# Keys in one written order, the output bias copied by ScalarE, low-rank products and step sizes with features on partitions, and an earlier loop entry, in a twelve-layer decoder kernel

## The chip, the cores and the metric

The kernel runs on one core of a Trainium2 chip. The time is that of the device for one launch, in microseconds (us); the profiled execution is one launch recorded instruction by instruction. The core has TensorE (PE; its weight loads are listed apart as PEld), VectorE (DVE), ScalarE (ACT), GpSimd (POOL) and SyncE (SP), each with a queue that it works off in order. They wait for one another by semaphores. All data are float32 if nothing else is said.

## The reference, cut to what matters

The program is a decoder of four blocks of three layers (attention, cross attention to a context, feed-forward), with a layer norm ahead of each layer and x = x + layer(norm(x)). x is 8 batches of 128 tokens by 256 features, the context 8 by 128 by 128. The change touches four layers: the third block's three and the fourth block's attention.

Third block, attention (`L2_attn`): a recurrence over tokens, with a rate for each head.

```python
q, k = elu(xWq) + 1, elu(xWk) + 1
kv_t = decay * kv_{t-1} + k_t * v_t ; ks_t = decay * ks_{t-1} + k_t
out = (q * kv / clip(sum_head(q * ks), 1e-6)) @ w_out
```

Third block, cross attention (`L2_xattn`): 16 heads of 16; the last 16 tokens of the context have weights and biases of their own and a softmax of their own; queries and keys are layer-normed by head.

```python
k = _ln((y_main @ Wk + bk).reshape(..., H, HD), kn_w, kn_b)
k_dca = _ln((y_dca @ Wk_dca + bk_dca).reshape(..., H, HD), kn_dca_w, kn_dca_b)
ctx = _attn(q, k, v) + _attn(q, k_dca, v_dca)
return ctx @ Wo + bo
```

Third block, feed-forward (`L2_ffn`): a base product, a shared product of rank 16 and six routed ones of rank 16, two of which count for a token.

```python
gates = softmax(x @ W_router + b_router) ; top two kept as w_per_e
h = einsum('bsd,edr->bser', x, A_r) * w_per_e[..., None]
return x @ W_base + b_base + (x @ A_s) @ B_s + einsum('bser,erf->bsf', h, B_r)
```

Fourth block, attention (`L3_attn`): a state space layer with 64 heads of 64 and a state of 128. z, x, B, C and dt are products of the normed input; x, B and C pass a causal convolution of four taps and a silu.

```python
dt = softplus(dt + dt_bias) ; dA_cs = cumsum(dt * A) over 128 tokens
L[i, j] = exp(dA_cs[i] - dA_cs[j]) for j <= i
Y = einsum('bcign,bcjgn,bcijgh,bcjghp->bcighp', Cm, Bm, L, dt * x) + D * x
return rmsnorm(Y * silu(z)) * norm_w @ W_out
```

## The kernel before, in words

x lies in SBUF as 128 tokens (partitions) by 8 batches by 256 features. A norm works in two halves of four batches: `norm_stats` (L144) takes statistics on VectorE, has ScalarE do a Ln and an Exp for the inverse root (L125, L126), corrects it in three small VectorE steps (L129 to L131) and writes `xn` (L165). `norm` (L172) turns `xn` with TensorE into `xnT` (features on partitions) and copies it out of PSUM, by turns with ScalarE and VectorE (L60, L62). `add_x` (L191) adds a result to x on VectorE.

Two things set the order of work. Inside `manual_schedule` (and so in `in_step`, L376) the instructions of each engine keep the order written down; outside of it, a planner orders them by its own costs, and it may mix them between those of written orders. `in_step` runs a list of stages, each with a lag, over blocks.

*Keys of the cross attention* (`L2Keys.keys`, L1521) are made at the end of the first feed-forward layer with experts (`l1_ffn`), while its last results come back from memory (y, L1298). There are two written orders: `Decay` and `rest` (parameters turned to columns, the value bias passed through Wo to `bo`), then four rounds of `project` (TensorE; ScalarE copies with bias, L1555, and squares, L1617), sums by head on TensorE, Ln and Exp (L1623, L1624), and `scaled`, a multiply on GpSimd (L1562). After them, outside of a written order, VectorE adds y to x and norms it. `masked` and `values` come later, in the steps of `l2_attn` (`late`).

*Recurrence* (`l2_attn`): four steps (two halves by two groups of features), each with three products, the scans on VectorE (L1392, L1393) by the rates of `Decay`, sums by head (L1412), inverse, spread (L1427) with `feats`, output.

*Cross attention* (`l2_xattn`): eight blocks through a pipeline of stages. `bias` (L1759) adds `bo` to x on GpSimd; it needs only that the norm has read x.

*Low-rank feed-forward* (`l2_ffn`, L1770): norm, with the base bias added to x by GpSimd (L188); router; softmax; `top2`; then for each of eight blocks a product x by A (128 tokens by 112), its weighting on VectorE (L1801), a transpose, a copy, and base product and low-rank product into one bank. It has no written order.

*State space layer* (`l3_attn`, L1817): norm, then one written order. The entry (L2014 to L2097) computes the step sizes with tokens on partitions (eight times two matmuls of 64 columns), softplus by Abs, Exp, Ln, Exp, a cumulative sum as a matmul with a triangle, a turn of the sums, their split into three bfloat16 parts, and writes the parts to memory (`parts`, L2057) to read them back as `own` (L2062) and, two blocks at a time, `upto` (L1912, `sums`); `decay` (L1917) then has TensorE form the differences and ScalarE bring them to SBUF. Beside that B and C are projected, convolved (`last_tap` on ScalarE, three `taps` on VectorE) and multiplied (`gT`), and the first two feature blocks are prepared. The loop (L2102) then runs fifteen passes over pairs of blocks. PSUM has two banks each with the names xz (products, differences) and ty (turns, results), and four with the name o.

## Time and profile before

| what | value |
|---|---|
| median of 3 runs | 1963.13 us (1957.91 to 1964.25) |
| profiled execution | 1960.42 us, span 1958.6 us |
| granted TensorE clock, mean of the span | 0.943 |
| busy: PE, DVE, ACT, POOL | 1712.1, 1203.2, 1034.0, 376.1 us |

By stage, from the busy times in stretches of the trace (us):

| stretch | what runs | PE | DVE | ACT | POOL | clock |
|---|---|---|---|---|---|---|
| 885 to 905 | keys, y added, norm | 12.0 | 14.6 | 8.8 | 8.1 | 0.83 |
| 905 to 940 | recurrence | 33.2 | 27.7 | 22.4 | 2.6 | 1.00 |
| 940 to 972 | its end, queries | 20.3 | 19.7 | 11.3 | 6.0 | 1.00 |
| 1000 to 1060 | cross attention | 53.4 | 39.4 | 32.9 | 3.0 | 1.00 |
| 1060 to 1103 | low-rank feed-forward | 33.6 | 25.4 | 6.0 | 9.7 | 0.80 |
| 1103 to 1145 | entry of the state space layer | 35.9 | 22.5 | 21.4 | 2.6 | 0.88 |
| 1200 to 1250 | its loop | 49.8 | 33.1 | 37.5 | 0.0 | 1.00 |

A line of the timeline gives start, duration, engine, line, operation, output<-inputs, shapes, how many were merged, and in brackets how long the engine stood idle before it and for whom. A matmul in float32 appears as two records.

### The profile page before, as it was taken

To read this page: it belongs to the slowest core of one execution; us is meant where nothing else is said; L and a number is where in the kernel's file an instruction comes from. 1 tells how busy PE (TensorE), PEld (TensorE's weight loads), DVE (VectorE), ACT (ScalarE), POOL (GpSimd) and SP (SyncE) were. 2 spreads that over 40 slices of the span, in tenths; PEclk is the share of its full clock that TensorE was granted. 3 is DMA by queue.
4 is the path that set the end of the run, shared out by engine and by line. 5 is a ranking of instruction groups with operands and counts; after the bars stand their busy time and mean duration, and the time that the engine had idled before them with its cause. 6 is when DMAs were issued, how large, how long until landed. Compare 5 with 4: busy or idle time off the path is not lost.

```text
span 1958.6 us, 25273 instructions
## 1 busy us (share of the span) xinstructions
PE 1712.1 (87%) x9521; PEld 1136.4 (58%) x9527; DVE 1203.2 (61%) x2384; ACT 1034.0 (53%) x1703; POOL 376.1 (19%) x363
## 2 busy tenths in 40 slices
PE   6776968758999977997787889999999996999999
PEld 3453645535666654664466545555555556888667
DVE  4766777765677752327665576776776775445433
ACT  2446844435767641225463278777787763444432
POOL 3544532110122223332102000000000001334200
PEclk9897988878999998999998899999999998999999
DMA  4500036205000031111001011101011004000000
GB/s 135 176 25 1 2 116 202 97 1 215 1 12 6 12 128 64 47 40 49 16 1 36 2 49 34 34 18 33 17 34 34 18 1 162 1 1 1 1 1 22
DMA packets 39784, 90.28 MB, mean 46 GB/s; under 512 B 7904, under 2 KB 20320, under 8 KB 38000
## 3 DMA queue, kind: packets, MB, share of 16 engines
q1 hardware_dynamic: 32096, 69.56, 10.3%
q0 software_dynamic: 5472, 17.54, 3.0%
q8 instruction: 76, 1.25, 0.3%
q10 hardware_dynamic: 2096, 1.57, 0.3%
q14 instruction: 44, 0.36, 0.1%
HBM read 67.15 MB, written 21.51 MB: 45 GB/s over the span
## 4 chain that ended last, share of the span: by engine, by line
PE 67%; DVE 15%; ACT 11%; issue 3%; POOL 2%; DMA 1%; ACTq 0%; SPq 0%; DVEq 0%; POOLq 0%
PE ps_xz L46 9%; PE ps_o L46 7%; PE ps_o L2007 6%; PE ps_o L845 5%; PE ps_mm L46 5%; PE ps_q L46 5%; PE ps_h L46 4%; PE ps_u L46 3%; PE ps_sc L46 3%; PE ps_ty L46 2%; PE ps_y L46 2%; PE ps_xz L1924 2%; DVE mx L508 2%; PE ps_ty L1945 2%; PE ps_sc L206 2%
## 5 line engine op out<-in xcount | busy, mean ns | idle before, releaser
L46 PE MATMUL ps_xz<-xnT,wxz 128*128 128x512 f32 x512 | 236.3, 605 | 1.7 <-ACT zs L1983 1.5
L46 PEld LDWEIGHTS ps_xz<-xnT,wxz 128*128 128x128 f32 x512 | 92.9, 191 | 105.1 <-issue 101.2
L1904 DVE SCALAR_TENSOR_TENSOR xc<-pad,w,xc 128x1024 f32<-128x1024 f32 x96 | 123.0, 1282 | 28.6 <-ACT xc L1898 26.9
L2007 PE MATMUL ps_o<-wo,yg 128*128 128x256 f32 x512 | 126.3, 391 | 1.5 <-DVE yg L1986 1.5
L845 PE MATMUL ps_o<-wvo,uT 128*128 128x256 f32 x512 | 122.3, 383 | 0.0
L845 PEld LDWEIGHTS ps_o<-wvo,uT 128*128 128x128 f32 x512 | 98.2, 192 | 40.1 <-issue 29.8
L1927 ACT ACTIVATE ee<-ps_xz,sgn 128x512 f32<-128x512 f32 x128 | 87.5, 690 | 59.1 <-PE ps_xz L1924 59.0
L2007 PEld LDWEIGHTS ps_o<-wo,yg 128*128 128x128 f32 x512 | 92.3, 189 | 24.9 <-issue 12.8
L2285 POOL MEMSET gb<- 128x160 f32 x1 | 0.2, 231 | 504.4 <-PE ps_ty L46 504.4
L1947 DVE TENSOR_TENSOR dtx<-ps_ty,dt 128x512 f32<-128x512 f32 x64 | 41.4, 686 | 84.3 <-PE ps_ty L1945 84.1
L46 PE MATMUL ps_h<-moe,xT 128*128 x184 | 85.0, 605 | 0.9 <-DVE xT L1241 0.8
L1937 DVE TENSOR_TENSOR ee<-ee,gT 128x2048 f32<-128x2048 f32 x32 | 73.2, 2288 | 13.1 <-ACT ee L1933 13.1
L46 PE MATMUL ps_u<-pT,cx 128*128 128x512 f32 x128 | 69.1, 622 | 6.9 <-ACT pT L828 6.7
L944 ACT ACTIVATE s<-ps_sc,mx,rqs 128x128 f32<-128x128 f32 x128 | 48.1, 456 | 49.9 <-DVE rs_t L129 47.0
L952 POOL TENSOR_TENSOR s<-s,sums 128x512 f32<-128x512 f32 x32 | 33.2, 1039 | 209.6 <-DVE sums L951 66.3
L1933 ACT ACTIVATE ee<-ee,sgn 128x1024 f32<-128x1024 f32 x64 | 73.1, 1147 | 0.2
L509 POOL TENSOR_TENSOR s<-s,mx 128x2048 f32<-128x2048 f32 x16 | 57.8, 3610 | 53.8 <-DVE mx L508 53.8
L1255 DVE TENSOR_TENSOR h<-ps_h,sl 128x512 f32<-128x512 f32 x23 | 15.9, 691 | 82.3 <-PE ps_h L46 82.3
L46 PE MATMUL ps_ty<-ee,dtx 128*64 128x128 f32 x1024 | 63.0, 276 | 3.0 <-DVE ee L1937 3.0
L46 PEld LDWEIGHTS ps_q<-xnT,wqk 128*128 128x128 f32 x512 | 63.5, 196 | 2.8 <-DVE xnT L62 1.0
L46 PE MATMUL ps_q<-xnT,wqk 128*128 128x128 f32 x512 | 63.9, 280 | 0.6 <-DVE xnT L62 0.6
L46 PE MATMUL ps_q<-wq,xnT 128*128 128x512 f32 x128 | 63.1, 616 | 0.5 <-ACT xnT L60 0.5
(583 smaller groups left out, 4035.6 us busy)
## 6 DMA issues: line engine op xcount, KB each, us to landing
moe<-in_p SPq DMA_DIRECT2D x24, 512.0 KB
rows_in<-zero_rows POOLq DMA_DIRECT2D x1, 8385.0 KB, 34.8
wxz<-in_p9s SPq DMA_DIRECT2D x32, 256.0 KB
fold_vo<-in_p SPq DMA_DIRECT2D x8, 512.0 KB
wvo<-fold_out SPq DMA_DIRECT2D x16, 256.0 KB
wvo<-wvo SPq DMA_DIRECT2D x2, 2048.0 KB
wo<-in_p9s SPq DMA_DIRECT2D x16, 256.0 KB
st<-in_p SPq DMA_DIRECT2D x3, 1024.0 KB
```

What stands on the lines that cost most here:

```text
L46: nc.tensor.matmul(out, lhsT, rhs, start=(i == 0), stop=(i == len(pairs) - 1))
L206: k.nc.tensor.matmul(psc(r, n), q[rows], rhs, start=True, stop=True)
L508: nc.vector.tensor_reduce(mx, SC.pop(u).rearrange("p r (j t) -> p (r j) t", t=P), AX.X, ALU.max)
L509: nc.gpsimd.tensor_tensor(sv, sv, mx.unsqueeze(2).to_broadcast([P, 16, P]), ALU.subtract)
L845: k.nc.tensor.matmul(self.po[b], uT[:, j, :], self.wvo[:, 4 * hg + j, :], start=hg + j == 0, stop=hg + j == 6)
L944: nc.scalar.activation(s[:, j, :], psc[:, j, :], AF.Exp, scale=rs[:, j : j + 1], bias=mx[:, j : j + 1])
L1904: nc.vector.scalar_tensor_tensor(XC[n], (PAD[n] if n in PAD else pads[n % 2])[:, :, t : t + S], cw[:, n, t : t + 1], XC[n], ALU.mult, ALU.add)
L1927: nc.scalar.activation(e, pm, AF.Relu, scale=sgn[:, at : at + 1])
L1933: nc.scalar.activation(EE[n][:, h], EE[n][:, h], AF.Exp, scale=sgn[:, at : at + 1])
L1937: nc.vector.tensor_tensor(EE[n], EE[n], gT.unsqueeze(1).to_broadcast([P, 2, B, S]), ALU.mult)
L1947: nc.vector.tensor_tensor(DTX[n][:, bs], pt.rearrange("p (b h d) -> p b h d", b=4, d=HD), dt_[:, bs, 2 * n : 2 * n + 2].unsqueeze(3).to_br ...
L2007: nc.tensor.matmul(PO[b // 2][:, b % 2 * D : (b % 2 + 1) * D], YG[n][:, tok(b)], WO[n // 2][:, n % 2, :], start=False, stop=n == 31 and b ...
```

## The change

- `norm_turned` is split from `norm`, so that halves can be turned where a written order wants it, in a bank of its choice.
- Keys: `Decay`, the parameters and the four rounds stand in one written order. Squares are kept in four buffers, `root` (head sums, Ln, Exp) is apart from `project`, and `scaled` multiplies on VectorE; the last two multiplies move into steps 1 and 2 of the recurrence (`late`). The second part of `Decay` (rates, `feats`) becomes `Decay.rest` and moves into the recurrence's step 0.
- Cross attention: before each GpSimd add, ScalarE copies `bo` into `row`, and the stage stands behind exp.
- Low-rank feed-forward: one written order. x by A is formed with features (112) on partitions, 512 tokens at a time; weights by token are spread to 112 columns, turned, and multiplied in. The base bias is row 113 of the last product, against a row of ones. Base products start their bank early and the low-rank product ends it. The next norm's halves stand in this order.
- State space layer: step sizes with heads on partitions, 64 rows for each half of the tokens (bias and A as columns `hcol`), softplus with Relu in it, the cumulative sum as a scan on VectorE that starts afresh every 128 tokens, no turn before the split. Parts are written by two DMAs and read back in two portions, the first for blocks 0 and 1 alone. dt is turned to tokens on partitions beside other work. The taps, differences and silu of block 1 move into the first pass of the loop; sgn moves to GpSimd.

```diff
+    def norm_turned(self, g, xnT, bank=None):
+        for c in range(NC):
+            pt = bank().rearrange("p (j t) -> p j t", t=P) if bank else self.trt()
+            for j in range(4):
+                self.nc.tensor.transpose(pt[:, j, :], self.xn[:, 4 * g + j, c * P : (c + 1) * P], self.ident)
+            self.evac(xnT[:, c, g * 512 : (g + 1) * 512], pt.rearrange("p j t -> p (j t)"))
...
+        self.own = tile_("own4", 4)
+    def rest(self):
+        k, nc, dec, heads, feats, own = self.k, self.k.nc, self.dec, self.heads, self.feats, self.own
+        nst = k.c[:, C_NST : C_NST + S].unsqueeze(1).to_broadcast([P, 4, S])
+        for o in range(NC):
+            nc.vector.tensor_scalar(self.rates[:, o, :, :], nst, dec[:, o : o + 1], None, ALU.mult)
...
+            (0, lambda s: project(s, 1, K)), (0, keys), (0, lambda s: k.decay.rest() if s == 0 else None),
+            (0, lambda s: project(s, 2, V)), (1, sums), (1, last(inverse)), (1, last(weigh_last)), (3, last(stats)), (0, scan),
...
+        self.kb = keep.tile([P, NC, 2, T], F32, name="kb")
+        self.kc = pool.tile([P, 4, 4, S], F32, name="kc")
+        self.rs = {}
+        with k.tc.manual_schedule():
+            k.decay = Decay(k, pool)
+            self.spread([self.bv[:, 0:8], self.bv[:, 8:16], *self.norms[2:4]])
+            self.project(0)
+            self.turn(4, 4, k.trt())
+            bv = pool.tile([P, NC, P], F32, name="bvT")
+            for o in range(NC):
...
+            self.spread([self.bq_row[:, o * P : (o + 1) * P].rearrange("p (h d) -> p h d", d=16) for o in range(NC)])
+            self.project(1)
+            self.turn(8, 2, k.trt())
+            self.root(0)
+            po = k.ot()
+            mm(nc, po, [(bv[:, o], self.wo[:, o, :]) for o in range(NC)])
+            nc.vector.tensor_tensor(self.bo, po, self.bo_row, ALU.add)
+            self.scaled(0)
+            self.project(2), self.root(1), self.scaled(1), self.project(3), self.root(2), self.root(3)
...
+        self.rs[u] = self.pool.tile([P, 4 * S], F32, name="sq", bufs=4)
+        nc.scalar.activation(self.rs[u], self.kc[:, u].rearrange("p b s -> p (b s)"), AF.Square)
+    def root(self, u):
+        k = self.k
+        pv = k.mmt()
+        mm(k.nc, pv, [(k.c[:, C_BO16 : C_BO16 + P], self.rs[u])])
+        l2_root(k, self.rs[u], pv)
+    def scaled(self, u):
+        rs = self.rs.pop(u).rearrange("p (b s) -> p b s", s=S)
+        self.k.nc.vector.tensor_tensor(self.kc[:, u], self.kc[:, u], rs, ALU.mult)
...
+        if u in (1, 2):
+            self.scaled(u + 1)
...
-            nc.gpsimd.tensor_tensor(k.x[:, b, :], k.x[:, b, :], l2k.bo, ALU.add)
+            row = wa.tile([P, D], F32, name="row")
+            act(row, l2k.bo)
+            nc.gpsimd.tensor_tensor(k.x[:, b, :], k.x[:, b, :], row, ALU.add)
         in_step(
             k, B,
-            (1, bias), (0, score), (3, turn_out), (0, later), (1, turn_p), (3, project), (0, maxima),
-            (3, lambda b: k.add_x(b, PY.pop(b))), (1, values), (0, less_max), (1, copied), (0, exp), (0, later_normed),
+            (0, score), (3, turn_out), (0, later), (1, turn_p), (3, project), (0, maxima),
+            (3, lambda b: k.add_x(b, PY.pop(b))), (1, values), (0, less_max), (1, copied), (0, exp), (0, later_normed), (1, bias),
...
-    wB = w[0:N, o_ : o_ + D]
+    wB = w[0 : N + 1, o_ : o_ + D]
+    nc.sync.dma_start(wB[N : N + 1], a["r8"][0:D].rearrange("(o d) -> o d", o=1))
...
+        hT = [wk_.tile([N + 1, HALF], F32, name=f"hT{g}") for g in range(2)]
+        wt = [wk_.tile([P, 4, 1 + E, R], F32, name=f"wt{g}") for g in range(2)]
+        for g in range(2):
+            nc.gpsimd.memset(hT[g][96:], 1.0)
+            nc.gpsimd.memset(wt[g][:, :, 0, :], 1.0)
+        probs = wk_.tile([P, B, 8], F32, name="probs")
...
+            def base(some):
+                for b in some:
+                    PY[b] = k.mmt((P, D))
+                    for c in range(NC):
+                        nc.tensor.matmul(PY[b], xnT[:, c, tok(b)], wb[:, c, :], start=c == 0, stop=False)
+            pl = k.ot((P, B, E))
+            def route(g):
+                k.norm_turned(g, xnT)
+                for b in range(4 * g, 4 * g + 4):
+                    mm(nc, pl[:, b, :], [(xnT[:, c, tok(b)], wr[:, c, :]) for c in range(NC)])
+            def small(g):
+                pu = U[g] = k.ot((P, HALF))[0:N]
+                mm(nc, pu, [(wa[:, c, :], xnT[:, c, g * HALF : (g + 1) * HALF]) for c in range(NC)])
+            route(0)
+            route(1)
+            nc.vector.tensor_tensor(lg, pl, br.unsqueeze(1).to_broadcast([P, B, E]), ALU.add)
+            softmax_small(k, lg, probs[:, :, 0:E])
+            for g in range(2):
+                small(g)
+                u = wk_.tile([N, HALF], F32, name=f"u{g}")
+                nc.scalar.copy(u, U[g])
+                U[g] = u
+            _, hots = top2(k, probs)
+            nc.vector.tensor_tensor(hots[0], hots[0], hots[1], ALU.add)
+            k.normed = 0
+            for g in range(2):
+                some = slice(4 * g, 4 * g + 4)
+                nc.vector.tensor_tensor(
+                    wt[g][:, :, 1:, :],
+                    hots[0][:, some, 0:E].unsqueeze(3).to_broadcast([P, 4, E, R]),
+                    probs[:, some, 0:E].unsqueeze(3).to_broadcast([P, 4, E, R]),
+                    ALU.mult,
+                )
+            base((0, 1))
+            for g in range(2):
+                pt = k.trt((P, 4, P))[0:N]
+                for i in range(4):
+                    nc.tensor.transpose(pt[:, i, :], wt[g][:, i].rearrange("p e r -> p (e r)"), k.ident)
+                nc.vector.tensor_tensor(hT[g][0:N], U[g], pt.rearrange("p i t -> p (i t)"), ALU.mult)
+            base((2, 3))
+            for g in range(2):
+                if g == 1:
+                    base(range(4, 8))
+                for i in range(4):
+                    b = 4 * g + i
+                    nc.tensor.matmul(PY[b], hT[g][:, tok(i)], wB, start=False, stop=True)
+                    k.add_x(b, PY.pop(b))
+                NORM[g] = k.norm_stats(g)
+                if g == 0:
+                    NORM[0]()
+            NORM[1]()
...
+        hcol = tile_([2], "hcol", 1, wp)
+        for g in range(2):
+            nc.sync.dma_start(hcol[g * H : (g + 1) * H], a["r9"].rearrange("(k h) -> h k", h=H))
...
+            starts = tile_([2, 4, S], "sq", 2)[:, 0]
+            nc.gpsimd.memset(starts, 1.0)
+            nc.gpsimd.memset(starts[:, :, 0:1], 0.0)
+            ze, ul, da = (tile_([2, 512], "yg", 4) for _ in range(3))
+            z, e, u, l = ze[:, 0], ze[:, 1], ul[:, 0], ul[:, 1]
+            pz = bank("ty")
+            for g in range(2):
+                k.norm_turned(g, xnT, lambda: bank("ty"))
+                mm(
+                    nc, pz[g * H : (g + 1) * H],
+                    [(wbc[:, c, 256:320], xnT[:, c, g * 512 : (g + 1) * 512]) for c in range(NC)],
+                )
+            nc.scalar.activation(e, pz, AF.Abs, bias=hcol[:, 1:2])
+            nc.scalar.activation(e, e, AF.Exp, scale=-1.0)
+            nc.vector.tensor_scalar(u, e, 1.0, None, ALU.add)
+            nc.scalar.activation(z, pz, AF.Relu, bias=hcol[:, 1:2])
+            nc.scalar.activation(l, u, AF.Ln)
+            nc.vector.scalar_tensor_tensor(e, u, 1.0, e, ALU.subtract, ALU.subtract)
+            nc.scalar.activation(u, l, AF.Exp, scale=-1.0)
+            nc.vector.tensor_tensor(z, z, l, ALU.add)
+            nc.vector.tensor_tensor(e, e, u, ALU.mult)
+            nc.vector.tensor_tensor(z, z, e, ALU.subtract)
+            cs, rest = da[:, 0], da[:, 1]
+            nc.vector.tensor_scalar(cs, z, hcol[:, 0:1], None, ALU.mult)
+            nc.vector.tensor_tensor_scan(rest, starts.rearrange("p b s -> p (b s)"), cs, 0.0, ALU.mult, ALU.add)
+            for n in (32, 33):
...
+            split = wk_.tile([P, 3, 512], BF16, name="zs", bufs=4)
...
+            for g in range(2):
+                (nc.sync, nc.gpsimd)[g].dma_start(
+                    parts[:, :, 4 * g : 4 * g + 4].rearrange("q h b s -> h q (b s)"), split[g * H : (g + 1) * H]
                 )
-            for q in range(3):
-                nc.sync.dma_start(
-                    own[3 + q * 2 * B : 3 + (q + 1) * 2 * B],
-                    parts[q].rearrange("(n h) b s -> (h b) n s", h=2),
-                )
-            for n in range(2):
-                sums(n)
-            for n in range(2):
-                x(n, 0), x(n, 1), last_tap(n)
+            for n in (slice(0, 2), slice(2, H // 2)):
+                for q in range(3):
+                    (nc.gpsimd if q == 1 else nc.sync).dma_start(
+                        own[3 + q * 2 * B : 3 + (q + 1) * 2 * B, n],
+                        parts[q].rearrange("(n h) b s -> (h b) n s", h=2)[:, n],
+                    )
+                if n.start == 0:
+                    sums(0), sums(1)
+            x(0, 0), x(0, 1), last_tap(0)
...
+            pt = bank("ty")
+            for i in range(4):
+                nc.tensor.transpose(pt[:, i * P : (i + 1) * P], z[:, i * P : (i + 1) * P], k.ident)
+            nc.scalar.copy(
+                dt_.rearrange("p (g b) h -> p b g h", g=2), pt.rearrange("p (b g h) -> p b g h", b=4, g=2)
+            )
+            x(1, 0), x(1, 1), last_tap(1)
...
+            gate(0, 0), gate(0, 1)
+            taps(32, range(3))
+            silu(32)
+            gate(1, 0), gate(1, 1)
+            taps(33, range(3))
+            silu(33)
+            taps(0, range(3))
...
+            for i in range(4):
+                decay(0, i)
+            silu(0), weighted(0), weighted(1)
...
+                if p == 1:
+                    taps(1, range(3))
+                    for i in range(4):
+                        decay(1, i)
...
+                if p == 1:
+                    silu(1)
```

## The prediction

> **What bounds the kernel now.** I read the page first: the busy shares, and the chain that ended last.
>
> ```profile
> PE 1712.1 (87%) x9521; PEld 1136.4 (58%) x9527; DVE 1203.2 (61%) x2384; ACT 1034.0 (53%) x1703; POOL 376.1 (19%) x363
> ...
> PE 67%; DVE 15%; ACT 11%; issue 3%; POOL 2%; DMA 1%; ACTq 0%; SPq 0%; DVEq 0%; POOLq 0%
> ```
>
> TensorE bounds the whole; the third of the chain that lies elsewhere is where stages meet, and every changed line is at such a border between 880 and 1175 us. So I read the timeline there, engine by engine. First VectorE and GpSimd where the keys are made:
>
> ```profile
> 896.94 1.31 POOL L1562 TENSOR_TENSOR kc<-kc,rs 128x512 f32<-128x512 f32 x1 [6.28 <-ACT rs L1624]
> 897.13 1.40 DVE L192 TENSOR_TENSOR x<-y,x 128x256 f32<-128x256 f32 x1
> 901.57 0.16 DVE L129 TENSOR_TENSOR rs_t<-ln 128x4 f32<-128x4 f32 x1 [0.96 <-ACT ln L126]
> 902.18 1.27 POOL L1562 TENSOR_TENSOR kc<-kc,rs 128x512 f32<-128x512 f32 x1 [3.94 <-ACT rs L1624]
> 902.38 1.08 DVE L131 SCALAR_TENSOR_TENSOR ln<-rs_t,ln 128x4 f32<-128x4 f32 x1
> 903.55 1.34 DVE L165 TENSOR_SCALAR xn<-x,ln_mv,ln 128x256 f32<-128x256 f32 x4
> 905.82 2.65 POOL L1562 TENSOR_TENSOR kc<-kc,rs 128x512 f32<-128x512 f32 x2 [2.37 <-ACT rs L1624]
> 907.26 1.24 DVE L129 TENSOR_TENSOR rs_t<-ln 128x4 f32<-128x4 f32 x1 [0.41 <-ACT ln L126]
> 950.23 2.20 DVE L165 TENSOR_SCALAR xn<-x,ln_mv,ln 128x256 f32<-128x256 f32 x4
> 950.72 2.97 POOL L1760 TENSOR_TENSOR x<-x,bo 128x256 f32<-128x256 f32 x4 [42.25 <-DVE xn L165]
> ```
>
> The reader is to see that a VectorE operation on SBUF lasts until GpSimd's multiply ends: L129 on 4 columns takes 0.16 alone and 1.24 beside it, four L165 take 1.34 alone and 2.20 beside L1760. Then the low-rank stage's small steps, and TensorE's clock in stretches of 4 us (the column after the five engines is the granted clock):
>
> ```profile
> 1073.14 0.21 DVE L1786 TENSOR_TENSOR lg<-ps_o,r 128x48 f32<-128x48 f32 x1 [3.35 <-PE ps_o L46]
> 1077.57 0.21 DVE L1795 TENSOR_TENSOR wt<-hot,probs 128x48 f32<-128x48 f32 x1
> 1098.11 0.42 DVE L192 TENSOR_TENSOR x<-ps_o,x 128x256 f32<-128x256 f32 x1 [0.86 <-PE ps_o L46]
> 1100.96 1.38 DVE L165 TENSOR_SCALAR xn<-x,ln_mv,ln 128x256 f32<-128x256 f32 x4
> ...
> 1104.00:1108.00 4.00, 4.00 (x20) 4.00 (x20) 0.00 (x0) 0.00 (x0) 0.00 (x0) 0.50 0.01 2
> 1108.00:1112.00 4.00, 4.00 (x15) 2.97 (x15) 0.69 (x1) 0.83 (x2) 0.00 (x0) 0.50 0.00 0
> ```
>
> and, from the chain, the way into the last attention's loop:
>
> ```profile
> 1103.51 6.87 PE ps_ty L46 x32
> 1110.38 8.80 PE ps_xz L46 x16
> 1119.18 0.87 PE ps_ty L46 x2
> 1120.07 0.70 DVE yg L2044
> ```
>
> The eight blocks of the low-rank stage take 20.5 us (1077.6 to 1098.1), each a round of TensorE, VectorE, TensorE, VectorE. The step sizes then hold TensorE for 6.87 us at half clock, and the loop (first L1945) starts only at 1146.95.
>
> **The change part by part.** Minus is a gain.
>
> *Keys.* From the landing of y (first add at 891.60) to the end of the second half's L165 (908.92+1.38=910.30) VectorE is the engine waited for. Taking kc from GpSimd removes the stretches above: 1.40-0.39, 1.08-0.16 and 1.24-0.16, together 3.0. The set order runs ScalarE's key work without the 5.81 us that L1555 waited at 894.08, when its matmul stood behind one that needed VectorE: about 13 us of ScalarE work (six pieces L1502 0.25, four times L1555 0.84, L1617 0.63, L1623 0.69, L1624 0.63) from 882.6 ends near 896, so the waits of 0.96 and 0.41 for the norm's Ln go too. Two multiplies are added on VectorE, 0.69 each by L1399, the nearest SBUF by SBUF row of that shape: +1.4. Sum -3.0; bounds -5 (the first half's norm also early) and 0 (multiplies and adds queue badly: the free part between the written orders is placed by a planner).
>
> *Decay's rest.* Rates (two 0.45), own (0.16 each without GpSimd) and feats (two 0.64) are 2.5 us of VectorE that lay under the wait for y; now they stand in the recurrence's first step, ahead of the scan, and two transposes (0.2) between two projections. Two more kc multiplies (1.4) come in steps 1 and 2. From 905 to 940 us VectorE is busy 27.7 of 35, so 7.3 us idle cover 3.9; the first consumer, L1412, started at 919.93 with its input ready at 917.5, 2.4 us of slack. I take +0.5, nearest to that slack; bounds 0 and +3.9 with the cover gone.
>
> *Output bias.* L1760 no longer runs beside the two L165 at 950.23 and 958.71, both in the chain: 2.20 to 1.38, twice, -1.6 (bounds -1.7 and 0). In exchange eight ScalarE copies of 128x256 (0.37 by L1749, 0.48 by L1990) stand behind each exp; behind it ScalarE is idle 0.55 before L1749 in most steps, so 0, bound +3.2 if none is covered. The GpSimd adds (0.75 each) now fall beside VectorE operations that read PSUM; two L192 took 0.74 beside L1760 and 0.75 alone, so 0.
>
> *Low-rank stage.* The base bias moves into the last matmul as a row of ones, so GpSimd's eight L188 go, and the L165 at 1066.12 shrinks by 0.8: the routing ends at 1072.3. I walk the queues from there. lg to the summed choice took 1073.14 to 1077.57, 4.4, so 1076.7; two weights of 128x384 at 0.56 (between L192's 0.42 for 256 columns and 0.69 for 512): 1077.9. TensorE meanwhile runs both 112x512 products and two base products: 3.44 at half clock, then 1.72+1.72: 1079.2. Four transposes 0.5, multiply 0.69, second group 0.69: 1081.1; base products 2, 3 to 1081.9. Four last products (0.43) and adds: 1084.1. Statistics of four blocks 2.1, variance 0.2, ScalarE 0.5, three small steps 0.5, L165 1.4: 1088.9. Four more adds 1.6 (their base products, 3.44, lie beside the statistics), statistics 2.1, then 1.2 and L165 1.4: 1095.2 against 1102.34. That is -7.1; bounds -9 (rounds fully beside each other) and -4 (products at half clock throughout).
>
> *Step sizes and loop entry.* The new product has as much TensorE time: four products of 512 columns at 0.86 are 3.44, where 32 records of 0.215 were 6.87 at half clock, or 3.44 at full. One bank holds its result, so the turned halves share the other: two rounds of 0.5 and 0.62 each, and half the clock at first, for TensorE idles about 5 us; result at 1104.0 (1101.9 with no half clock, 1105.0 with it and the copies in the other order). Then Abs, Exp, Relu, Ln, Exp (0.63 each), 0.43, three times 0.69, 0.43, a scan 1.2 (1.22 by L1392) and 0.43+0.69+0.43+0.69+0.43: splits done 9.0 later, before 14.2, with the triangular matmul and its copy gone. Reading back: two writes (0.6 to issue, 3.8 to land), own for two blocks, sums (2.3 to land): 8.5, ready at 1121.5; first use at 1130. That queue is SP's, with load(1) last in it: weights by 1124, needed at 1135. From the product on ScalarE has the five steps, eight copies 0.57, four taps 1.24, dt 0.6, the Silu table 1.28, four gates 0.58, two silus 1.04, L1927 four times 0.60, silu(0) 1.04: 22.4, and 7.6 of waits, as TensorE's twelve products of 1.72 pass to it through two xz banks. The loop starts at 1134.1, before 1146.95. The first pass has more: three taps 1.29, four decays, four L1927, a silu, of which ScalarE's 3.4 count: second pass at 1162.2, where before it was 1173.92. The same walk with the old order gives 1147.3 and 1173.9. Less the 7.1 above: -4.6; bounds -6.8 and -2.5.
>
> Moved at no cost: sgn, memsets and GpSimd's share of own, since GpSimd is idle from 1076.3 to 1124.9; without that cover about 1 us. The hcol loads sit on SP at 1055, 50 us early.
>
> Sum: -3.0+0.5-1.6-7.1-4.6 = -15.8. The profiled execution took 1960.42 (span 1958.6): 1944.6. It is 2.7 below the median 1963.13 of runs from 1957.91 to 1964.25, by which it would be 1947.3; I say 1946.
>
> **Rivals.** (a) The gains at the last border are paid back in the first pass: decay(1), silu(1) and the Exp table queue on ScalarE, which there is busy from 1150.4 to 1162.0 nearly without a gap. With that term at 0: 1949 to 1952. For it: that row; against it: the walk, which has these pieces in it.
>
> (b) The low-rank order does not overlap with what follows: VectorE's copies of the turned first half come behind the second half's norm, and each half waits for all of the other. The two terms vanish, 11.7 us: 1956 to 1959, no change. Against it: at 1063.53 an L62 copy ran between L155 of an earlier written order, so orders do mix.
>
> (c) Slower: TensorE's half clock. The new orders leave it three waits (before the weights, before the second norm, before the loop's first transposes). Before, spells at 0.50 to 0.59 lasted from 1066 to 1084 and from 1104 to 1114. If the 31 us of dense products from 1072 to the loop (13.8+3.4+13.8) all ran at half clock, where I count 5 us of that, it costs 25: 1970. From 16 us of extra time on, it decides. Against it: dense 512-column work brought 1.00 back by 1116.
> The Trainium skill, page "TensorE: Matmul & The Clock Gate", section "Part 1: The HAM clock gate", says that one busy window of about 3.4 us releases the clock again. By that rule a wait costs 1.7 us at most, three 5, an estimate from its window: 1951. The trace differs: the clock stayed 0.50 from 1104 to 1112 with TensorE busy 4.00 of 4.00, in records of 64 columns.
>
> **How the numbers follow.** Forecast 0.62, (a) 0.16, (b) 0.12, (c) 0.10. All bounds low: 1960.4-5-1.7-9-6.8 = 1938, with 0.2% of run spread 1934. All high: 1960.4+0+3.9+3.2-4-2.5 = 1961, which (b) stays under. So 1934 to 1961. Under 0.3% (6 us) cannot be told from no change. Faster: forecast, (a) and a little of (b), 0.80; same: most of (b), some of (c), 0.11; slower: 0.09.
>
> **What would show it.** No VectorE row above 0.2 for L129 and L131's 4 columns near 900; L165 four in 1.4 at 950; the last add of the low-rank stage by 1091, not 1098; first L1945 transposes (their new line) some 13 us earlier, second pass 12. Wrong if the clock column is 0.5 through the products, if ScalarE's exp in the first pass starts as late as before, or if the recurrence's first scan waits for the rates.

## The result, and the profile after

The changed kernel takes 1954.26 us in the median of 18 runs (1948.35 to 1958.27); the kernel before, run on the same chip, 1965.18 (18 runs, 1957.91 to 1968.18). The ratio is 0.995, with a 95% interval of 0.9939 to 0.9961: about 10 us faster, where the sum of the prediction was 15.8. The profiled execution took 1957.12 us, its span 1955.3. It is only 3.3 shorter than that of before: it is itself 2.9 above its median, and the profile of before is 4.8 below its own (1960.42 against 1965.18). The first changed line alone comes 4.1 us later in it (first add of y at 895.72, before 891.60) although nothing above was changed; in the twelve profiles of the experiments this mark lies anywhere from 889.4 to 894.2. So I measure from mark to mark inside each profile. From the page, the busy shares and the engines of the chain that ended last:

```profile
PE 1717.8 (88%) x9471; PEld 1136.2 (58%) x9477; DVE 1203.0 (62%) x2374; ACT 1037.7 (53%) x1711; POOL 365.8 (19%) x359
...
PE 68%; DVE 14%; ACT 11%; issue 3%; POOL 2%; DMA 1%; ACTq 0%; DVEq 0%; SPq 0%; POOLq 0%
```

TensorE bounds it as before. The stretches (us; each the difference of two start or end times in the timelines):

| | stretch | before | changed | difference | forecast |
|---|---|---|---|---|---|
| A | first add of y to the first transposes with the heads | 28.33 | 27.95 | -0.4 | -2.5 |
| B | last of these to the first score maxima | 28.57 | 27.51 | -1.1 | -1.6 |
| C | first maxima to the first exponent | 8.66 | 10.40 | +1.7 | 0 |
| D | first exponent to lg | 92.02 | 91.80 | -0.2 | -0.8 |
| E | lg to the last low-rank add's end | 25.39 | 18.02 | -7.4 | |
| F | that to the end of the splits | 26.05 | 19.77 | -6.3 | |
| G | splits to the loop's first transposes | 22.37 | 20.64 | -1.7 | |
| H | loop's start to its first output product | 31.75 | 34.73 | +3.0 | |
| | E to H together | 105.56 | 93.16 | -12.4 | -10.9 |
| I | first output product to the last score of the last attention | 649.41 | 650.58 | +1.2 | 0 |
| | A to I, with the unchanged recurrence | 936.51 | 925.37 | -11.1 | -15.8 |
| J | from there to the last add | 127.26 | 130.93 | +3.7 | 0 |

A to I fits the 10.9 us between the medians. I and J have the same code in both kernels; J is the last feed-forward. Now the timeline of the changed kernel where the keys are made, VectorE, GpSimd, ScalarE and TensorE:

```profile
889.97 3.64 POOL L1541 MEMSET va<- 128x1024 f32 x4
889.39 4.51 DVE L1348 COPY own<-consts 128x4 f32<-128x4 f32 x1
889.50 4.52 DVE L1554 TENSOR_SCALAR bvT<-consts,prm 128x128 f32<-128x128 f32 x2
894.01 2.08 PE L46 MATMUL ps_o<-w,bvT 128*128 128x256 f32 x4 [2.23 <-DVE bvT L1554]
897.94 0.84 ACT L1582 ACTIVATE kc<-ps_mm,prm 128x448 f32<-128x448 f32 x2 [4.76 <-PE ps_mm L46]
904.52 0.16 DVE L129 TENSOR_TENSOR rs_t<-ln 128x4 f32<-128x4 f32 x1
905.35 0.15 DVE L131 SCALAR_TENSOR_TENSOR ln<-rs_t,ln 128x4 f32<-128x4 f32 x1
906.20 1.76 PE L191 MATMUL ps_tr<-consts,xn 128*128 128x128 f32 x8 [2.53 <-DVE xn L165]
908.61 3.78 PE L46 MATMUL ps_mm<-xnT,w 128*128 128x512 f32 x4 [0.65 <-DVE xnT L62]
909.95 1.38 DVE L165 TENSOR_SCALAR xn<-x,ln_mv,ln 128x256 f32<-128x256 f32 x4
912.19 1.78 PE L191 MATMUL ps_tr<-consts,xn 128*128 128x128 f32 x8
915.18 1.29 DVE L1351 TENSOR_TENSOR feats<-ps_tr,own 128x512 f32<-128x512 f32 x2 [0.60 <-PE ps_tr L1346]
916.39 0.68 DVE L1384 SCALAR_TENSOR_TENSOR k<-e,z 128x512 f32<-128x512 f32 x1
```

L129 and L131 take 0.16 and 0.15, and VectorE's last L165 ends 15.6 us after the first add of y (before 18.7): the -3.0 of the prediction is there. But the first k follows that end by 5.1 us, before by 1.7, and the gain is gone. Two things stand in between: transposes and products at half clock (four records of 512 columns take 3.78), and feats ahead of k. And two of VectorE's operations on SBUF last 4.5 us, until GpSimd's four fills are done.

The lines that answer to the other rows shown of before:

```profile
953.98 1.38 DVE L165 TENSOR_SCALAR xn<-x,ln_mv,ln 128x256 f32<-128x256 f32 x4
975.15 2.35 DVE L1713 TENSOR_REDUCE mx<-ps_sc 128x16 f32<-128x1792 f32 x2 [2.21 <-PE ps_sc L209]
975.02 3.72 PE L46 MATMUL ps_q<-xnT,w 128*128 128x512 f32 x4
1077.35 0.21 DVE L1841 TENSOR_TENSOR lg<-ps_o,r 128x48 f32<-128x48 f32 x1 [3.25 <-PE ps_o L46]
1087.51 1.72 DVE L195 TENSOR_TENSOR x<-ps_mm,x 128x256 f32<-128x256 f32 x4 [1.24 <-PE ps_mm L1871]
1093.96 1.41 DVE L195 TENSOR_TENSOR x<-ps_mm,x 128x256 f32<-128x256 f32 x4
1099.27 1.39 DVE L165 TENSOR_SCALAR xn<-x,ln_mv,ln 128x256 f32<-128x256 f32 x4
1102.76 2.95 PE L46 MATMUL ps_ty<-xnT,w 128*64 128x512 f32 x4
```

L165 is at 1.38 where it was 2.20; behind it the four query products take 3.72, at half clock, where they took 1.98 before (972.32). The low-rank adds come four at a time. The last four records of the step sizes hold TensorE for 2.95 us; the first four (1.07 twice) ran ahead of the second half's norm, where the 32 records of before took 6.87 after it. The granted clock in two places, in stretches of 3.41 us (after span, PE, PEld, DVE, ACT and POOL comes the clock):

```profile
968.32:971.74 3.42, 1.80 (x8) 0.48 (x10) 0.75 (x1) 2.44 (x5) 0.00 (x0) 1.00 0.00 0
971.74:975.15 3.41, 2.24 (x17) 0.87 (x16) 0.75 (x1) 1.24 (x2) 0.00 (x0) 0.50 0.00 0
975.15:978.56 3.41, 3.41 (x4) 1.04 (x4) 3.41 (x3) 0.00 (x0) 0.00 (x0) 0.50 0.00 0
978.56:981.98 3.42, 2.64 (x7) 1.06 (x6) 1.21 (x2) 1.95 (x3) 0.00 (x0) 1.00 0.00 0
...
1859.20:1862.60 3.40, 3.40 (x12) 2.12 (x11) 1.30 (x5) 0.36 (x1) 0.00 (x0) 0.50 0.00 0
1862.60:1866.00 3.40, 3.40 (x9) 1.85 (x8) 0.58 (x2) 0.69 (x1) 0.00 (x0) 0.50 0.01 2
```

The half clock begins at 971.7 and ends at 978.6, two stretches. In the last feed-forward (1859) the changed kernel's profile has four such stretches (13.7 us), that of before two (6.8): that is J, and the last section shows it over fourteen profiles. I is longer for the same reason: this profile has one more stretch of half clock in it (from 1606.6, 20.5 us in all against 17.1). In the seven profiles with 17.1 us there, I takes 648.8 to 649.4 us, in the six with 20.5 it takes 650.6 to 651.1, and in the one with 23.9 it takes 650.5.

### The profile page after: what moved, and what is told of

It reads as the page before. It is cut to its first block, busy times and chain, and to the rows that moved or that the text cites. A ratio compares the mean times of both kernels' runs of the same rounds, so it can differ in the third digit from the quotient of the medians.

```text
span 1955.3 us, 25181 instructions
## 1 busy us (share of the span) xinstructions
PE 1717.8 (88%) x9471; PEld 1136.2 (58%) x9477; DVE 1203.0 (62%) x2374; ACT 1037.7 (53%) x1711; POOL 365.8 (19%) x359
## 3 DMA queue, kind: packets, MB, share of 16 engines
q10 hardware_dynamic: 2096, 1.57, 0.3%
## 4 chain that ended last, share of the span: by engine, by line
PE 68%; DVE 14%; ACT 11%; issue 3%; POOL 2%; DMA 1%; ACTq 0%; DVEq 0%; SPq 0%; POOLq 0%
PE ps_xz L46 9%; PE ps_o L46 7%; PE ps_o L2077 6%; PE ps_o L848 5%; PE ps_mm L46 5%; PE ps_q L46 5%; PE ps_h L46 4%; PE ps_u L46 3%; PE ps_sc L46 3%; PE ps_y L46 2%; PE ps_ty L46 2%; PE ps_xz L1994 2%; DVE mx L511 2%; PE ps_ty L2015 2%; PE ps_sc L209 2%
## 5 line engine op out<-in xcount | busy, mean ns | idle before, releaser
L358 PE MATMUL ps_tr<-consts,s 128*128 128x128 f32 x384 | 55.7, 290 | 8.4 <-ACT s L1726 3.3
```

Source lines behind the costliest of these rows:

```text
L358: k.nc.tensor.transpose(pt[:, r, :], src(g)[:, r, :], k.ident)
```

## The experiments

No kernel here leaves out work; four of them add useless products, as their edits show.

**One part alone.** Each part on the kernel before. `keys_only`:

```diff
 # on the kernel before
-    with k.tc.manual_schedule():
-        k.decay = Decay(k, pool)
-        self.rest()
...
+    with k.tc.manual_schedule():
+        k.decay = Decay(k, pool)
+        self.spread(...), self.project(0), self.turn(4, 4, k.trt())
...
+    (0, keys), (0, lambda s: k.decay.rest() if s == 0 else None),
```

> The kernel before with the keys' part of the change alone: one written order, the multiply on VectorE, the rest of Decay in the recurrence's first step. In the changed kernel VectorE's copy `own` (128x4) and the two bvT operations took 4.5 us each and ended with GpSimd's four fills of va (889.97 to 893.61), TensorE's product with bvT waited 2.23, and the keys' chain on ScalarE 4.76. Theory (GpSimd's fill holds VectorE's operations on SBUF): the same here, with nothing of the other parts present: from the first add of y to the recurrence's first transposes with the heads 28.0 us (changed kernel 27.95, kernel before 28.3), ScalarE's wait for the third projection near 4.8, whole time 0 to -0.5 us. Rival (the fills and probs memsets that GpSimd takes in for the low-rank stage, or another part, disturb it): without them the interval is 25.8, as the prediction's -2.5 says, and the whole time -2.5 us.

A is 27.49 (-0.8): the own copy takes 4.52 and ScalarE waits 4.77 here too, with no other part present, so that rival falls. VectorE's last L165 ends 15.2 us after the first add. B and C together are 3.7 longer, with half clock from 959.6 to 963.0 and 969.8 to 976.7. The whole took 1961.46 (12 runs), ratio 0.9986 (0.9972 to 0.9999).

`bias_only`:

```diff
-            nc.gpsimd.tensor_tensor(k.x[:, b, :], k.x[:, b, :], l2k.bo, ALU.add)
+            row = wa.tile([P, D], F32, name="row")
+            act(row, l2k.bo)
+            nc.gpsimd.tensor_tensor(k.x[:, b, :], k.x[:, b, :], row, ALU.add)
...
-    (1, bias), (0, score), (3, turn_out), ...
+    (0, score), (3, turn_out), ... (0, exp), (0, later_normed), (1, bias),
```

> The kernel before with the output bias alone moved behind the exponent (ScalarE's copy, GpSimd's add). Both L165 ahead of the queries go from 2.20 to 1.38, the first score maxima come 1.6 earlier. Theory (the clock's fall is a matter of where its windows lie): the 1.6 stay, or are lost, by whether TensorE's clock falls to 0.5 in the second half's query products, as it did from 972 to 978 in the changed kernel; where it falls, the first exponent comes no earlier (0 to +0.2), where not, 1.6 earlier. Rival (the copies on ScalarE cost): 8 copies of 0.4 lengthen the loop's period of 8.93 by up to 0.4, +3.2 us by the loop's end. Whole time -1.6 to 0 by the theory, +1.6 by the rival.

TensorE's timeline of this kernel:

```profile
967.77 0.71 PE L209 MATMUL ps_sc<-kb,qT 32*128 32x256 f32 x8 [1.58 <-ACT qT L1665]
968.42 3.65 PE L46 MATMUL ps_q<-xnT,w 128*128 128x512 f32 x4
```

And its stretches of 4 us, clock in the same column as above:

```profile
964.00:968.00 4.00, 1.64 (x14) 0.54 (x16) 0.75 (x1) 2.68 (x4) 0.00 (x0) 1.00 0.00 0
968.00:972.00 4.00, 4.00 (x12) 1.26 (x8) 3.44 (x3) 0.00 (x0) 0.00 (x0) 0.57 0.00 0
```

B is 26.92 (-1.65, the forecast's -1.6), C is 10.33 (+1.67): the gain is there at the maxima and is given back at once by one window of half clock on the query products (3.65 where 1.98 stood before). D is 92.04 (before 92.02), so ScalarE's copies cost nothing; the whole is 0.9998 (0.9986 to 1.0011).

`ffn_only` and `entry_only`:

```diff
 # ffn_only: only l2_ffn of the change
+    hT = [wk_.tile([N + 1, HALF], F32, name=f"hT{g}") for g in range(2)]
...
 # entry_only: only l3_attn of the change
+    k.norm_turned(g, xnT, lambda: bank("ty"))
+    mm(nc, pz[g * H : (g + 1) * H], ...)
```

> The kernel before with the low-rank stage's part alone. Theory: the stage from lg to the last add shrinks from 25.0 to about 17.6 us as in the changed kernel (-7.4), and as the following norm is inside the order, the norm's end another 0 to 1 earlier; whole time -7 us. Rival (the stage's gain needs the new loop entry behind it, which takes the turned halves one after the other): the old entry turns both halves only after the second norm, and gives back 1 to 3: whole time -4 to -6.

E is 18.28 (-7.1), F gives back 1.6 (27.69), with 13.7 us of half clock from 1096.1 where the kernel before had 10.2, and E to H is -5.8. That is the rival's -4 to -6 at this mark. D is 1.8 shorter as well, with 9.5 us of half clock in it where the kernel before had 13.7. The whole is 0.9961 (0.9945 to 0.9976), which does not tell theory and rival apart.

> The kernel before with the step sizes by head and the early loop entry alone. Theory: from the last low-rank add to the loop's first transposes 48.8 us become 40.8 as in the changed kernel, and the first pass pays 3 back on ScalarE (block 1's decays and gates are in it), so the first output products come 5.1 earlier and the whole time is -5. Rival (a), the first pass pays all back: whole time 0. Rival (the entry gains only with the low-rank order, whose norm of the first half is early): -2 to -3.

F is 16.38 instead of 26.05, H is 34.61 (+2.9), E to H together -8.5, the whole 0.9973 (0.9958 to 0.9988), so at these marks neither rival holds. The entry gains more alone than in the changed kernel, where both parts together make -12.4, 1.8 less than the sum 5.8 + 8.5. With the old low-rank order the adds come block by block, so that most of the second half's statistics are done when the last add ends, and its L165 ends 3.4 us after that (1101.89). With the new one the last four adds come at once (1093.96), all four statistics follow them, and L165 ends 5.3 us after the last add. These 1.9 us are the difference.

**The keys.** `fill_later` moves the fills of va behind the written order:

```diff
-        for b in range(0, B, 2):
-            k.tc.keep_in_program_order(nc.gpsimd.memset(self.va[...], 0.0))
         with k.tc.manual_schedule():
             k.decay = Decay(k, pool)
...
+        for b in range(0, B, 2):
+            k.tc.keep_in_program_order(nc.gpsimd.memset(self.va[...], 0.0))
```

> The changed kernel with one thing moved: GpSimd's four fills of va stand behind the written order of the keys, not ahead of it (the kernel before had them behind its first order too). Theory (the fill holds VectorE's operations on SBUF for as long as it runs): own 128x4 at 0.2 and bvT at 0.6 instead of 4.5 each, TensorE's product with bvT near 890.5 instead of 894.0, ScalarE's wait of 4.76 for the third projection below 1.5, and from y's first add to the recurrence's first transposes with the heads 25.5 us instead of 27.95 (the prediction's -2.5); whole time -2.5 us. Rival (the written order itself queues badly: TensorE at half clock, feats and the heads' transposes ahead of k): the short operations are short, but the interval stays above 27.

```profile
883.81 0.55 DVE L1348 COPY own<-consts 128x4 f32<-128x4 f32 x1
883.92 0.60 DVE L1550 TENSOR_SCALAR bvT<-consts,prm 128x128 f32<-128x128 f32 x2
888.03 0.84 ACT L1582 ACTIVATE kc<-ps_mm,prm 128x448 f32<-128x448 f32 x2 [0.42 <-PE ps_mm L46]
900.34 1.97 PE L191 MATMUL ps_tr<-consts,xn 128*128 128x128 f32 x8 [7.01 <-DVE xn L165]
902.88 3.78 PE L46 MATMUL ps_mm<-xnT,w 128*128 128x512 f32 x4 [0.57 <-DVE xnT L62]
```

The fills were what held VectorE: 0.55 and 0.60, and ScalarE's wait is 0.42. (The 0.55 that is left ends with the DMA instruction L1278 that GpSimd is issuing, at 884.4.) But A is 27.54, 0.4 shorter, and not 2.5: my theory had the stall right and its price wrong. The keys are done seven microseconds before the norm, TensorE waits 7.01 us, and its clock is halved from 894.3 to 907.9. The whole was 1949.16 (6 runs), 0.9922 (0.9900 to 0.9945), of which the 0.4 explains little; A to I together are 925.34, as in the changed kernel (925.37).

`feats_early` puts Decay's rest into the keys' order of `fill_later`:

```diff
             nc.vector.tensor_tensor(self.bo, po, self.bo_row, ALU.add)
+            k.decay.rest()
             self.scaled(0)
```

> fill_later, with Decay's rest (rates, own, the heads' transposes, feats) back in the keys' written order instead of the recurrence's first step. In fill_later VectorE's last L165 ends 15.2 us after y's first add (18.7 in the kernel before: the -3.0 of the prediction is there), but the first k comes 5.0 after that end, where it came 1.7 after it before; feats (1.29) and the wait for the heads' transposes stand ahead of k. Theory (Decay's rest is on the chain, the slack that the prediction counted on is not there): y's first add to the first transposes with the heads 26.2 us instead of 27.54. Rival (it lies in a wait that TensorE's half clock makes anyway): within 0.3 of 27.54.

It went the other way, A 28.75. VectorE's timeline:

```profile
893.27 1.43 DVE L195 TENSOR_TENSOR x<-y,x 128x256 f32<-128x256 f32 x4 [5.95 <-DMA y<-rows_out]
...
894.96 0.41 DVE L1560 TENSOR_TENSOR bo<-ps_o,r 128x256 f32<-128x256 f32 x1
895.28 0.87 DVE L1343 TENSOR_SCALAR dect<-consts,dec 128x512 f32<-128x512 f32 x2
...
897.09 1.29 DVE L1351 TENSOR_TENSOR feats<-ps_tr,own 128x512 f32<-128x512 f32 x2
```

VectorE stands 5.95 us idle and then does all of it behind y's first adds, because the bo add, in the written order ahead of it, was placed behind them. Its way to the last L165 grows to 17.4, and k comes 2.3 behind that end instead of 5.0. So Decay's rest does cost some 2 us in either place. The half clock stands in this A too, from 896.4 to 913.5, after a wait of TensorE of 9.19 us. The whole: 0.9936 (0.9914 to 0.9959).

This profile settles another question. It has no half clock in B and C, although the code of the queries is that of the changed kernel:

```profile
972.84 1.98 PE L46 MATMUL ps_q<-xnT,w 128*128 128x512 f32 x4
971.48:974.89 3.41, 2.63 (x12) 0.99 (x12) 1.91 (x1) 0.69 (x2) 0.00 (x0) 1.00 0.00 0
```

B and C together are 35.66 here, 1.57 less than the 37.23 of before: the forecast's 1.6 for the output bias in full. With one stretch of half clock there they take 37.0 to 37.3 (`bias_only`, `multiply_gpsimd`, `filled_keys`, `combined`), with two 37.9 (the changed kernel, `fill_later`, `block1_ahead`).

`filled_keys` fills TensorE's wait in `fill_later` with useless products:

```diff
             self.project(2), ..., self.root(2), self.root(3)
+            idle = k.mmt((P, 4, S))
+            for i in range(15):
+                nc.tensor.matmul(idle, k.c[:, C_BO16 : C_BO16 + P], k.ctxT[:, 0:4, :], start=True, stop=True)
```

> fill_later, with 15 useless products of 512 columns (6.5 us at full clock) behind the last sum of squares of the keys, where TensorE is idle for 7.0 us until the first half's norm. In fill_later TensorE ran at half clock from 894.3 to 907.9, four windows of 3.41: the first half's turn took 1.97 (8 transposes) and the first four products 3.78, twice what they take at full clock. Theory (the keys that are done early leave TensorE idle, and the half clock behind that takes the gain back): clock 1.00, 3.78 becomes 1.9, 1.75 becomes 1.0, and the interval of 27.54 becomes 25.5 to 26. Rival (VectorE's order and feats set it): 27.2 or more.

```profile
910.09 1.09 PE L191 MATMUL ps_tr<-consts,xn 128*128 128x128 f32 x8
911.53 1.09 PE L191 MATMUL ps_tr<-consts,xn 128*128 128x128 f32 x8 [0.35 <-DVE xnT L62]
912.46 1.88 PE L46 MATMUL ps_mm<-xnT,w 128*128 128x512 f32 x4
```

I had sized them wrongly: a float32 product is two records, the fifteen took 13.0 us, and the turn waited for them until 910.09; A is 29.07. What lies behind them ran at full clock: 1.09 and 1.88 where 1.97 and 3.78 stood. So the half clock follows from the idle time, as the theory had it: `combined`, with the same fifteen products, has none in A either, `last`, with seven, one stretch, `fill_later` with its wait of 7.01 us four and `feats_early` with 9.19 five. The gain of the interval was not shown by this kernel. The whole: 0.9946 (0.9923 to 0.9968).

`multiply_gpsimd` gives the first two multiplies of the changed kernel back to GpSimd:

```diff
-        self.k.nc.vector.tensor_tensor(self.kc[:, u], self.kc[:, u], rs, ALU.mult)
+        eng = self.k.nc.gpsimd if u < 2 else self.k.nc.vector
+        eng.tensor_tensor(self.kc[:, u], self.kc[:, u], rs, ALU.mult)
```

> The changed kernel with the first two multiplies of kc on GpSimd again. Theory (the prediction's price of two engines on one buffer): VectorE saves two times 0.69 and pays up to 1 us for each operation that stands beside a multiply of 1.3, so y's first add to the first transposes with the heads 0 to +1.6 over 27.95; rows of VectorE that end with the GpSimd row are to be seen. Rival (taking the multiply to VectorE only costs VectorE's time): 1.4 shorter.

```profile
890.64 1.31 POOL L1595 TENSOR_TENSOR kc<-kc,sq 128x512 f32<-128x512 f32 x1
890.07 2.50 DVE L195 TENSOR_TENSOR x<-y,x 128x256 f32<-128x256 f32 x4 [1.64 <-DMA y<-rows_out]
893.15 1.41 DVE L195 TENSOR_TENSOR x<-y,x 128x256 f32<-128x256 f32 x4
```

Beside the multiply four adds take 2.50, alone 1.41, and a single add beside the second 1.21 against 0.39: 1.9 lost for 1.4 of multiplies saved. VectorE's way to the last L165 is 15.7 against 15.6, A 27.91 against 27.95. At these two places the engine of the multiply is of no account; the rival (1.4 shorter) falls. The whole: 0.9943 (0.9922 to 0.9963).

**The queries.** `filled_queries` puts two useless products ahead of each sum of squares:

```diff
     pv = (bank or k.mmt)((P, n))
+    for rhs in fill:
+        nc.tensor.matmul(pv, k.c[:, C_BO16 : C_BO16 + P], rhs, start=True, stop=True)
     mm(nc, pv, ...)
```

> The changed kernel with two useless products of 512 columns (0.43 each) into the bank of each sum of squares of the queries, in TensorE's wait of 0.78 for ScalarE's squares, so that TensorE is busy nearly without a gap before the score's maxima. It adds work and takes none away. Theory (the 1.7 us that the first exponent lost against the first maxima are TensorE's half clock from 972 to 978, and the idle before it brings that): clock 1.00 there, the way from the first maxima to the first exponent 8.7 to 9.2 us instead of 10.40; whole time -1 to -1.5. Rival (the clock falls by a fixed pattern whatever TensorE does, or the loss is a wait): 10.4 to 10.8, whole time +0.4.

C is 11.39 and B 28.23: the theory's numbers fail. The products were twice as long as I had counted (1.72 a pair in a wait of 0.78), and there was still one window of half clock, 970.9 to 974.3 (two in the changed kernel), behind the two score batches, where nothing had been filled in. That the half clock takes the gain is shown by `feats_early`, and not by this kernel. The whole: 0.9955 (0.9932 to 0.9978).

**The first pass.** `block1_ahead`:

```diff
             for i in range(4):
                 decay(0, i)
             silu(0), weighted(0), weighted(1)
+            taps(1, range(3))
+            for i in range(4):
+                decay(1, i)
+            silu(1)
...
-                if p == 1:
-                    taps(1, range(3))
-                    for i in range(4):
-                        decay(1, i)
...
-                if p == 1:
-                    silu(1)
```

> The changed kernel with block 1's taps, four decays and silu ahead of the loop again. Theory (the first pass pays back on ScalarE what block 1's work would cost ahead of it): the loop starts some 3.4 us later (four Relu of 0.6 and a Silu of 1.04), the way from its start to the first output product shrinks from 34.7 to 31.8 us, whole time within 1 us of the changed kernel. Rival (the first pass is slow for another reason: the second portion of own, the clock's fall at 1135): the way stays at 34.7, whole time +3.4. Rival (early start is a gain in full): whole time +3 with the way at 31.8.

G is 23.11 (+2.5), H 31.51 (-3.2), I 648.95 (-1.6, but `multiply_gpsimd`, without this edit, has 648.86: both lack the stretch of half clock that the changed kernel's profile has at 1606.6). ScalarE's timeline of the changed kernel, where block 1's four Relu stand among the exponents:

```profile
1140.66 1.15 ACT L2003 ACTIVATE ee<-ee,sgn 128x1024 f32<-128x1024 f32 x1
1141.90 0.59 ACT L1960 COPY pad<-ps_xz 128x512 f32<-128x512 f32 x1
1142.38 3.63 ACT L1997 ACTIVATE ee<-ps_xz,sgn 128x512 f32<-128x512 f32 x6
1145.90 1.24 ACT L1968 ACTIVATE xc<-pad,w 128x1024 f32<-128x1024 f32 x1
```

The six Relu, block 1's four and two that the pass always has, hold ScalarE for 3.63. With block 1 ahead the loop starts 2.5 later and its first output product comes 0.7 earlier. These 0.7 are not the edit's: with 3.4 us of half clock in G and H each, `filled_keys` (block 1 in the pass) takes 54.18 for both together and `combined` (block 1 ahead) 54.22. Entering the loop early is paid back in full; the gain of the entry lies in the step sizes. That ScalarE is the engine on which it is paid is read from its rows; no run changes ScalarE's part alone. The whole: 0.9932 (0.9909 to 0.9954).

**Together.** `combined` takes fills later, `feats_early`, the fifteen products and block 1 ahead; `last` has Decay's rest ahead of the product with bvT, seven products, and useless products ahead of block 0's two score batches:

```diff
+            k.decay.rest()
             po = k.ot()
...
+            for i in range(7):
+                nc.tensor.matmul(idle, ...)
...
+                for r, at in ([(0, 0)], [(r, 256) for r in range(3)])[o] if b == 0 else []:
+                    nc.tensor.matmul(psc[:, r, at:512], ..., xnT[:, 0, at:512], start=True, stop=True)
```

> The changed kernel with four edits together: fills later, Decay's rest early, useless products in the idle time behind the keys, block 1 ahead of the loop. If the two causes in the keys add, y's first add to the first transposes with the heads is 24.2 to 24.7 us (27.95 in the changed kernel, 28.33 before). block1_ahead already reached the first output product 0.7 earlier than the changed kernel and lost another 0.9 less on the way to the last skip. Sum: -3.5-1.6 = -5 us against the changed kernel's whole time; less where the clock's windows fall otherwise, in steps of up to 3.4 us.

> Five edits on the changed kernel, each read in its own stretch. Fills later as in fill_later. Decay's rest in the keys' order, but ahead of the product with bvT, so that VectorE has it done before y lands (in feats_early it stood behind the bo add, which stood behind y's first adds, and VectorE's way to the last L165 grew from 15.2 to 17.4 us). Seven useless products behind the keys in place of 15 (each is two records of 0.43: the 15 took 13.0 us and held the first half's turn until 910.1, 6.5 us after its first L165; behind them the products ran at full clock). Useless products ahead of the two score batches of block 0 (0.86 and 1.3 in waits of 0.78 and 1.58). Block 1 ahead of the loop. Theory: y's first add to the last L165's end 15.2; from there to the first k 2.5 to 3 (5.0 in fill_later, 1.7 in the kernel before); first transposes with the heads 25 us after the first add (27.5 to 28 in the others); the last heads' transpose to the first exponent 36.2 to 36.8 (37.9 in the changed kernel, 37.2 before); loop start to first output 31.5. Together -3, -1 and -1.6 against the changed kernel, whole time -5 us. Rival (the clock's windows fall somewhere else and take it back): the first interval below 25.5, but a half-clock window more in a later stage, and whole time within 2 us of the changed kernel.

`combined`: A 28.83, for the two causes found under `feats_early` and `filled_keys`; E to H 92.43; whole 1946.97 (6 runs), 0.9917 (0.9891 to 0.9943). `last`: A 26.88, the shortest of all, but not 25: the two rates waited on the fills and on the fill of hT behind them (4.94 for 0.9 of work), so feats again ran behind y, and a window of half clock stood at 906.2. k comes 3.2 after the last L165. B and C are 38.14 (changed kernel 37.91): the half-clock window came at 967.6, before the filled places could act, and the fillers then ran in it. Whole 1947.52 (7 runs), 0.9953 (0.9935 to 0.9972). No variant is shown to beat the changed kernel: the interval of `combined` meets its own.

## Why the prediction was right, and where not

It said 1946 and got 1954.26, inside its range and on the right side, with two thirds of the gain that its sum had (10.9 of 15.8). The size alone would fit rival (a), whose sum is 15.8 - 4.6 = 11.2, but that is luck: E to H, where (a) has its loss, gained 12.4 and more than the forecast's 10.9, and the 4.7 us that A to I lack (11.1 of 15.8) are missing elsewhere: 2.1 in A, 2.3 in B and C, 0.6 in D and 1.2 in I, less 1.5 won in E to H. Step by step:

*Keys, -3.0.* Right for VectorE (18.7 to 15.6, no stretched L129 and L131) and wrong for the stage. The step that failed is the end of its chain: it stopped at the last L165 and took what follows as fixed. What follows grew from 1.7 to 5.1 us. By the lengths of the records some 1.9 of the four products and 0.7 of the transposes are half clock, which this term did not have: keys made early leave TensorE idle, while the late chain of before had kept giving it products until 905. The forecast used the clock only at the last border, in its terms there and as a rival. How the 3.4 us divide between the clock and feats is not shown: no kernel has A without the half clock and without a new delay. `last`, with one stretch of it, has the shortest A (26.88).

*Decay's rest, +0.5.* Mis-sized: feats (1.29) and 0.6 of wait for the heads' transposes stand straight ahead of k. The slack of 2.4 us was that of a later operation; the first one has none. The bound +3.9 held it. The rates and own, which the term also moved behind y, did not go there: they need nothing from y, and the planner placed them ahead of it (888.49 to 894.2).

*Output bias, -1.6.* Right as a mechanism and a size: 1.57 less in B and C where no half clock falls into them (`feats_early`), and the copies cost nothing. In the changed kernel's profile it is lost one step on: B is only 1.1 shorter, and C is 1.7 longer by half clock on the query products.

*Low-rank and entry, -11.7.* Right: -12.6 from the first exponent to the loop's first output product. Inside it, lg to the last L165 is 23.3 against 29.2 (-5.9; -7.1 was said with the 0.8 ahead of lg, of which D has 0.2), the loop's start is earlier than said (15.4 from lg, said 12.0) and the first pass longer (+3.0, said +1.1). Two of these numbers hold some clock: E to H have 13.8 us of half clock, before 27.2, of which the forecast counted the step sizes alone; and `filled_keys`, with 3.4 us of it in H where the changed kernel has 6.6, has 33.23 there and not 34.73. So rival (a) is half true: the early entry is paid back, as `block1_ahead` shows, but not the step sizes. Rival (b) is out: the first half's L165 stands at 1092.67, ahead of the last adds, and VectorE's copy of the turned first half at 1096.68, ahead of the second half's L165 (1099.27).

*Rival (c)*, half clock through the dense products, did not come: it stood until 1080.95, as the forecast had counted it for the first products, and then 3.4 us each at 1101.4, 1135.6 and 1145.8. But the same mechanism, in small, took most of what is missing: up to 2.6 us in A by the lengths of the records, 2.3 in B and C, 1.2 in I, and in that profile 3.7 in J. The Trainium skill, page "TensorE: Matmul & The Clock Gate", section "Part 1: The HAM clock gate", says that the clock is set by free-running windows of 3413 ns. The traces agree: from 880 us on each half-clock spell that the end of the program does not cut off lasts 3.4, 6.8, 10.2, 13.7 or 17.1 us, the two longer ones ahead of that 20.5 and 23.9 or 27.3, and the edges of one run lie on one grid (before, from 888.75 to 1144.75: 75 times 3.413). That a busy window releases it they show only with a reserve. In before these windows were full of records, and stayed at half clock:

```profile
1103.79:1107.20 3.41, 3.41 (x19) 3.41 (x18) 0.00 (x0) 0.00 (x0) 0.00 (x0) 0.50 0.01 2
1107.20:1110.61 3.41, 3.41 (x16) 3.41 (x16) 0.20 (x1) 0.00 (x0) 0.00 (x0) 0.50 0.00 0
1110.61:1114.03 3.42, 3.42 (x5) 1.35 (x5) 1.91 (x5) 2.21 (x4) 0.00 (x0) 0.50 0.00 0
1114.03:1117.44 3.41, 3.41 (x9) 1.47 (x8) 2.77 (x4) 2.41 (x4) 0.00 (x0) 1.00 0.00 0
```

In the first two the weight load is busy throughout (64-column records), in the third not, and the window after it is at full clock. That the gate counts work in the array and not busy records would fit; it is argued, not shown.

What stays open: why a given window falls. In the changed kernel TensorE was busy 1.80 of 3.42 us ahead of the fall at 971.7; in before 1.84 of 3.41 (967.26 to 970.67) brought none, nor did 1.78 of 3.42 in `feats_early` (968.06 to 971.48), with the same code.

## What to carry to other kernels

A chain is followed to its next consumer on the engine that bounds the kernel, and not to the end of the engine that was sped up: there one sees the small operation that was moved ahead of it and the clock that TensorE has by then. When an upstream stage ends earlier, ask what TensorE does in the time won; here a wait of 7 us put four stretches of half clock on the products around it, and seven or fifteen filled-in products brought that to one or none. Where windows of 3.4 us decide the clock, a change of 1 or 2 us is judged by marks inside the profile, between profiles that have the same half clock in the stretch; its share of the whole time may come out anywhere within a window or two.

## What was not expected of the hardware

- Four GpSimd fills in a row (3.64 us) held a VectorE copy of 128x4 and two tensor_scalar operations of 128x128 for 4.5 us, of which the first 0.6 passed beside the DMA instruction that GpSimd was issuing (888.93 to 889.96); a copy from PSUM took 0.15 beside the fills in the kernel before. The Trainium skill, page "SBUF — State Buffer", section "Who interferes with whom", says that copies and tensor_scalar operations can be shut out for as long as GpSimd holds the ports that both share; the trace agrees, and shows it over four instructions.
- The unchanged stretch J took 126.0, 127.3 to 127.6, 130.8 to 131.0 or 133.9 us in fourteen profiles, and its half clock sorts them without exception: 3.4 us at 126.0 (one profile), 6.8 at 127.3 to 127.6 (three), 13.7 at 130.8 to 131.0 (seven), 20.5 at 133.9 (three).
